# The sandwich kernel: the 1018 pieces of its first part in another order

## The chip, the cores and the metric

The kernel runs on one core of a Trainium2 chip. A core has five engines, each with its own in-order instruction queue: TensorE (PE in the profile; PEld is its weight load, which overlaps PE), VectorE (DVE), ScalarE (ACT), GpSimd (POOL) and SyncE (SP, which here only issues DMAs). Matrix products write into PSUM banks; DVE and ACT read them from there into SBUF. Engines wait for each other through semaphores. The metric is the device time of one execution in microseconds (us); times of several executions are given as a median.

## The reference, cut to what matters

Two batches of 2048 tokens with 256 channels pass through a first attention with three branches and then through two layers of local attention with a gated feed-forward network.

```python
h0 = layernorm(x, eps=1e-5)                              # (2, 2048, 256), input of the first part
gates = sigmoid(h0 @ Wg + bg); gates /= gates.sum(-1) + 1e-6
compressed = h0.reshape(2, 512, 4 * 256) @ Wc + bc        # one row for each 4 tokens
comp_out = attend(compressed)                            # 512 rows, put at the first 512 tokens
idx = sort(top_k(h0 @ Ws + bs, 128))                     # 128 tokens of each batch
sel_out = attend(h0[idx])                                # 128 rows, put at the first 128 tokens
win_out = attend(windows of 64 at stride 32)[:2048]      # first 2048 rows
out = 0.5 * (concat(comp_out*g0, sel_out*g1, win_out*g2) @ Wo + bo) + 0.5 * h0
x = x + layernorm(layernorm(out, eps=1e-6), eps=1e-5)    # end of the first part
y = layernorm(x, eps=1e-5)                               # input of the second part
for l in range(2):
    y = y + local_attention(shift(y) @ wqkv[l]) @ wo[l]  # 8 heads, blocks of 128, rotary with xpos
    a, g = split(layernorm(shift(y)) @ w1[l] + b1[l])
    y = y + (a * gelu(g)) @ w2[l] + b2[l]
result = x + layernorm(y, eps=1e-5)
```

`attend(t)` is softmax attention of t's queries against t's keys and values, with Wq, Wk, Wv.

## The kernel before, in words

The tokens lie as 8 groups g of 4 tiles of 128 rows (X[g] raw, Y[g] normed), 4 groups per batch. The kernel has two parts, with different PSUM pools: the first (lines 334 to about 905) has three banks pa, two pb, two pc and one po; the second has pa=2, pb=2, pc=4.

**How the first part is ordered.** A wrapper around the engines (class Engine, line 134, and class Notes, line 152) does not issue the operations of the first part when the code calls them; it notes them. Consecutive operations on one engine form a *piece*; `cut()` starts a new one, as does every step given to `do(f, ...)` (line 862). There are 1018 pieces. At the end

```python
with tc.manual_schedule():
    nc.give_out(int(i) for i in FIRST.split())
```

issues the pieces in the order in which their numbers stand in the string FIRST (line 41). Tiles and banks are taken when a piece is issued (class Later, line 104). No scheduler changes anything behind that, so the in-order queue of each engine is the subsequence of its own pieces in FIRST. In the profile every operation of the first part carries the line of give_out, L173, and every operation of the second part the line L147, so the tile names tell them apart.

**Steps of the first part**, with the pieces that the prediction speaks of:

- `first.turn` (53 on PE; 54, 55): turns the bias vectors, whose last row va waits for a DMA of bv; `later_on.turn` (223 on PE, 224 on DVE) does so for the second part.
- `open_moments(g)` (79 and 80 for g=1; 96/97, 114/115, 131/132, 148/149, 165/166, 183/184 for g=2 to 7): the statistics on DVE, then the reciprocal root and the shift on POOL. Group 0 has one such step for each tile (56 to 63).
- `open_norm(g)` (64 on DVE for g=0, 81, 98, 116, ... on ACT): X to Y.
- `open_turn(g)`: transposes of Y on PE in two halves (68 and 65 for g=0, 85 and 82 for g=1, ...), copies to xnT on DVE and ACT (66, 69, ...), and rearranged copies "perm" on POOL (70 and 67, 87 and 84, 104 and 101, 122 and 119).
- `open_products(g)`: gates and scores (71 and 73 for g=0, 88 and 90 for g=1, 106 and 108 for g=2) and the products of perm with Wc (75 and 77; 92 and 94; 110 and 112; 129 and 127), which give the compressed rows cT.
- `value_weights`, `value_biases` (205 to 222): products of Wv and Wo.
- the search for the 128 largest scores by counting, as rounds between DVE and PE (pieces 225 to 283 or so).
- `selected(b)` (line 686): numbers of the rows, an indirect DMA on POOL's queue that gathers them (330 for the second batch), their norm, transposes, queries, keys, values and attention (331 to 353 for the second batch).
- `compressed_open(b)` (line 665; 402 to 417 for the second batch): queries (406 on PE, 407 on DVE into qTc), keys (kTc), values (412 to 417, into cv). `compressed(b, i)` (line 674): scores (418 on PE for tile 0, 426, 434, 442 for the next), softmax and product.
- for each of 16 pairs i of windows: `win_qk`, `win_v`, `win_score`, `win_turn`, `win_out`, `win_add` and `win_close` (lines 735 to 860). `win_turn` turns the probabilities PW on PE to wpT, `win_out` multiplies them with the values VW and adds the result to Y (z) with statistics; `win_add` norms z on ACT, adds it to X on POOL and takes the statistics of X; `win_close` norms X to Y on ACT, the output of the first part. For pair 10, `win_add` is 833 to 840 (835 and 838 statistics on DVE, 839 on POOL, 840 on DVE) and `win_close` 841 and 842 on ACT; for pair 11 they are 864 to 871 (869, 871 on DVE, 870 on POOL) and 872, 873; for pair 15 `win_out` ends with 997 to 1002, `win_add` is 1003 to 1010, and `win_close` 1011 and 1012.

**The second part** has its own written-out order (a list of places with two more order strings), issued after the first. Its first operations turn tiles of Y on PE, copy them to h on ACT and multiply h with wqkv. The queues run on across the border, so ACT's first copy of h stands behind ACT's last piece of the first part.

Of the kernel before, what the change touches and what calls it, by code (L numbers as in the profile page):

```python
# [38 lines left out]


FIRST = """
2 27 6 3 23 0 1 4 5 7 8 9 10 56 205 24 11 40 25 60 12 57 13 58 14 61 62 15 16 206 59 26 63 64 68 17 28 79 65 69
70 53 66 18 80 19 54 55 71 20 21 22 72 67 81 29 73 74 30 85 96 31 75 86 87 32 77 114 97 33 82 98 78 115 83 102
34 76 148 84 116 88 35 99 92 131 149 36 89 103 37 90 94 104 150 93 91 100 38 132 105 165 120 39 117 121 41 219
101 133 42 106 43 95 122 118 44 112 45 183 46 107 119 220 47 48 110 166 49 50 113 51 52 184 108 1013 167 134 109
111 1014 123 135 1015 137 1016 136 1017 207 129 124 185 125 209 126 127 130 138 210 139 208 200 201 154 151 155
146 156 152 128 153 140 147 144 141 142 171 143 145 157 172 163 173 158 161 164 168 162 215 169 174 170 159 189
216 160 186 190 175 187 191 460 176 188 177 192 178 462 461 179 193 283 194 196 180 195 204 202 181 225 197 203
226 213 227 228 456 182 214 229 457 458 230 450 459 231 232 451 354 233 234 235 454 236 452 237 455 238 453 211
239 240 241 212 466 242 463 221 243 467 464 244 222 198 245 246 468 247 465 199 217 248 497 249 218 355 250 494  # L50
251 362 252 360 469 363 472 498 495 253 361 524 254 499 496 526 255 525 503 256 500 527 491 257 470 522 258 493
471 492 259 523 475 260 356 261 476 262 357 358 263 264 265 359 378 266 267 368 379 268 380 369 528 269 382 270
529 386 383 381 271 387 394 272 388 273 390 389 274 395 391 364 275 396 366 276 397 365 277 398 278 592 367 279
593 384 280 598 385 399 281 599 400 282 284 473 533 288 285 401 536 286 392 537 534 474 538 535 542 539 287 393
289 477 290 530 321 478 291 532 501 504 567 292 596 319 479 502 505 293 531 597 506 294 480 295 508 507 561 484
481 485 509 540 370 563 482 562 541 510 568 486 569 545 371 543 594 546 372 564 595 296 661 511 297 373 515 603
544 573 547 662 516 298 600 548 512 299 602 665 513 300 601 549 604 301 517 666 309 302 550 605 565 303 310 554
307 609 304 555 305 308 514 663 551 306 518 556 566 311 570 664 552 606 312 519 571 667 313 607 572 520 314 553
608 315 576 316 612 668 574 557 636 521 577 633 317 634 736 318 635 558 639 320 560 575 322 637 737 483 578 613
323 734 487 638 325 559 642 324 735 326 579 732 327 488 580 610 328 489 611 738 329 614 330 490 581 615 739 617  # L60
733 616 643 677 674 582 618 669 585 583 678 671 675 619 670 584 640 707 673 586 331 704 672 332 679 620 808 708
621 641 333 645 809 644 622 705 334 646 631 374 706 806 375 335 709 632 338 710 807 340 713 339 647 587 624 702
341 676 625 648 344 588 703 626 342 649 336 345 343 623 376 337 627 650 589 654 628 408 651 655 377 629 680 652
630 656 591 683 414 409 653 402 590 415 657 658 346 660 403 410 659 347 348 681 406 411 349 682 686 407 350 404
351 687 352 405 684 416 353 685 688 417 742 689 748 744 743 740 690 749 750 412 741 691 754 745 692 413 426 695
746 693 747 696 751 697 711 418 427 712 428 694 716 419 698 430 717 714 776 420 810 431 429 421 715 422 699 811
718 777 700 434 719 701 423 778 720 752 435 755 773 721 436 424 774 753 725 437 756 722 782 726 775 759 425 723
438 727 757 724 812 758 728 432 814 813 729 731 730 442 433 439 760 783 761 440 443 784 444 762 766 446 445 441
763 804 767 447 764 768 788 805 779 789 876 780 765 815 877 818 781 816 769 448 817 819 785 820 821 824 770 786
849 449 771 846 787 850 772 790 847 825 851 843 791 848 822 880 845 823 792 826 844 829 852 881 827 793 855 882  # L70
794 828 797 795 853 878 884 883 798 830 874 879 854 831 796 858 875 799 856 948 859 800 916 949 832 888 857 950
801 836 889 917 802 837 860 803 913 861 918 890 885 915 914 919 862 886 922 944 951 920 887 863 921 946 891 864
925 945 865 894 892 223 224 893 895 947 866 897 867 896 958 898 833 899 868 955 834 900 923 952 924 926 901 956
954 959 928 927 953 988 929 957 985 960 930 989 983 902 990 931 906 903 907 961 986 932 984 962 987 963 964 967
904 933 965 968 937 934 938 966 994 969 935 939 995 970 991 971 936 992 993 940 972 997 996 973 869 999 976 998
974 977 1000 870 941 978 1001 942 975 943 1002 979 871 1006 905 1003 1007 980 872 908 1004 981 1008 982 909 1005
873 838 1009 910 835 912 1010 911 839 1011 1012 840 842 841
"""


# [1374 lines left out]
```

## Time and profile before

| | us |
|---|---|
| time, median of 3 (lowest, highest) | 1560.8 (1560.66, 1562.59) |
| the profiled execution, its own time | 1561.83 |
| its span | 1560.1 |
| PE busy | 1502.4 (96%) |
| DVE busy | 1068.3 (68%) |
| ACT busy | 758.9 (49%) |
| POOL busy | 740.2 (47%) |
| granted PE clock, mean | 0.991 |
| last matmul of the first part ends | 228.12 |
| last ACT operation of the first part ends | 238.00 |
| first product with wqkv starts | 238.51 |

The profiled execution's time is 1.7 us more than its span, which runs from its first to its last instruction. How to read the profile: a line of the timeline has the start, the duration, the engine, the line, the operation, the tiles (out<-in) with their shapes, the count of operations run together, and in square brackets how long the engine had been idle and which operation released it. A line of the waits has the engine and tile that waited, the engine and tile waited for, and then the total, the number and the longest of these waits. In the page's slices each digit is the busy share of 1/40 of the span in tenths.

### The profile page before, as it was taken

How to read it: one execution, taken by the hardware profiler on the slowest of the kernel's cores; microseconds unless marked ns; L12 is line 12 of the kernel's file. 1: busy time of each engine (PE TensorE's matmuls, PEld its weight loads, DVE VectorE, ACT ScalarE, POOL GpSimd, SP SyncE). 2: the span in 40 equal slices, each digit the busy share in tenths (PEclk: the TensorE clock that was granted, in tenths of full speed). 3: DMA queues.
4: the chain of work that ended last, by engine and by line, in shares of the span. 5: the costliest groups of instructions: out<-in, count | busy, mean ns of one | idle time of the engine just before them, and what ended most of it. 6: DMA issues, size and time to landing. Idle time of an engine off the chain costs nothing.

```text
span 1560.1 us, 32507 instructions
## 1 busy us (share of the span) xinstructions
PE 1502.4 (96%) x12344; PEld 980.8 (63%) x12344; DVE 1068.3 (68%) x3139; ACT 758.9 (49%) x2213; POOL 740.2 (47%) x906
## 2 busy tenths in 40 slices
PE   7999967999999999999999999999999999999998
PEld 6877743566666666655555566666666665655554
DVE  6588784777888888844545368888888886454553
ACT  4336554677766776611111156677776765111110
POOL 7205256766666666510111166666666762232333
PEclk9999988999999999999999999999999999999999
DMA  7000001100000000101000010000000000001000
GB/s 227 1 1 8 1 18 37 33 6 8 5 9 5 8 5 8 52 8 28 14 17 0 1 41 30 9 5 9 5 9 5 6 8 8 15 31 31 21 24 31
DMA packets 32990, 30.76 MB, mean 20 GB/s; under 512 B 5634, under 2 KB 31172, under 8 KB 32836
## 3 DMA queue, kind: packets, MB, share of 16 engines
q1 hardware_dynamic: 32644, 28.17, 5.9%
q8 instruction: 98, 1.61, 0.4%
q0 software_dynamic: 192, 0.52, 0.1%
q14 instruction: 56, 0.46, 0.1%
HBM read 20.30 MB, written 4.19 MB: 16 GB/s over the span
## 4 chain that ended last, share of the span: by engine, by line
PE 76%; DVE 3%; POOL 2%; ACT 1%; issue 1%; DMA 0%; SPq 0%; POOLq 0%; ACTq 0%; DVEq 0%
PE pa L147 29%; PE pb L147 24%; PE pc L147 23%; DVE rr L147 1%; POOL rr L147 1%; DVE prob L147 1%; POOL ss L147 1%; DVE Y L147 0%; DVE hh L147 0%; ACT prob L147 0%; DVE ss L147 0%; ACT probT L147 0%; ACT sq L147 0%; DVE u L147 0%; DMA sh<-Y 0%
## 5 line engine op out<-in xcount | busy, mean ns | idle before, releaser
L147 PE MATMUL pa<-wqkv,h 128*128 128x512 f32 x768 | 370.3, 605 | 15.3 <-ACT h L147 11.3
L147 POOL TENSOR_TENSOR rr<-rr 128x256 f32<-128x256 f32 x256 | 184.4, 751 | 307.1 <-DVE rr L147 243.9
L147 ACT ACTIVATE ge<-pa,vb 128x512 f32<-128x512 f32 (+1 forms) x107 | 66.8, 626 | 363.1 <-PE pa L147 328.2
L147 ACT ACTIVATE prob<-prob,off 128x192 f32<-128x192 f32 (+2 forms) x512 | 224.8, 442 | 17.9 <-DVE off L147 17.0
L147 PEld LDWEIGHTS pa<-wqkv,h 128*128 128x128 f32 x768 | 132.1, 191 | 128.9 <-issue 104.3
L147 POOL TENSOR_TENSOR ss<-ss,mhalf 128x16 f32<-128x16 f32 x64 | 187.3, 2926 | 0.8
L147 ACT COPY probT<-pb 128x384 f32<-128x384 f32 (+1 forms) x256 | 119.2, 469 | 120.2 <-PE pb L147 117.2
L147 PE MATMUL pa<-hh,w 128*128 128x512 f32 x368 | 171.5, 593 | 0.0
L147 DVE SCALAR_TENSOR_TENSOR u<-pb,vb,ge 128x512 f32<-128x512 f32 x73 | 54.6, 751 | 165.0 <-PE pb L147 159.7
L147 DVE CUSTOM_DVE_ANT_0 prob<-pc,mask_loc 128x192 f32<-128x192 f32 (+2 forms) x512 | 148.8, 346 | 26.2 <-PE pc L147 20.4
L147 DVE TENSOR_TENSOR rr<-pa,cs 128x1024 f32<-128x1024 f32 x128 | 151.4, 1217 | 21.1 <-ACT sq L147 18.9
L147 PE MATMUL pc<-w,u 128*128 128x256 f32 (+1 forms) x896 | 164.6, 383 | 0.0
L147 PEld LDWEIGHTS pc<-w,u 128*128 128x128 f32 (+1 forms) x896 | 129.0, 173 | 47.8 <-issue 32.7
L147 PE MATMUL pb<-hh,w 128*128 128x512 f32 x292 | 137.3, 592 | 1.4 <-DVE u L147 1.4
L147 POOL TENSOR_TENSOR rr<-rr,ss 128x512 f32<-128x512 f32 x128 | 133.1, 1059 | 2.8
L147 DVE TENSOR_TENSOR prob<-prob,den 128x768 f32<-128x768 f32 x128 | 128.1, 1001 | 5.0
L147 PEld LDWEIGHTS pb<-ident,prob 128*128 128x128 f32 x752 | 87.9, 141 | 61.0 <-issue 31.2
L147 ACT ACTIVATE sq<-pa 128x512 f32<-128x512 f32 x128 | 75.6, 592 | 98.1 <-PE pa L147 93.5
L147 PE MATMUL pb<-ident,prob 128*128 128x128 f32 x752 | 118.3, 278 | 5.1 <-DVE prob L147 4.1
L147 PE MATMUL pb<-wo,oT 128*128 128x256 f32 x512 | 121.4, 380 | 0.2 <-DVE ss L147 0.2
L147 POOL TENSOR_SCALAR r<-mv 128x1 f32<-128x1 f32 (+1 forms) x48 | 9.3, 193 | 228.7 <-DVE mv L147 226.3
L147 PE MATMUL pc<-kr,qT 64*64 64x192 f32 (+2 forms) x2688 | 108.7, 287 | 2.2 <-ACT qT L147 2.2
(255 smaller groups left out, 2483.4 us busy)
## 6 DMA issues: line engine op xcount, KB each, us to landing
cs<-in_rope_dram SPq DMA_DIRECT2D x32, 128.0 KB
out_dram<-res SPq DMA_DIRECT2D x32, 128.0 KB
w<-in_L_ffn_w_dram SPq DMA_DIRECT2D x6, 640.0 KB
X<-_attn_hidden_states_dram SPq DMA_DIRECT2D x7, 512.0 KB
sh<-Y SPq DMA_DIRECT2D x16, 224.0 KB
wqkv<-in_L_ffn_wqkv_dram SPq DMA_DIRECT2D x2, 1536.0 KB
Wc<-in_L_attn_Wc_dram SPq DMA_DIRECT2D x1, 1024.0 KB
wo<-in_L_ffn_wo_dram SPq DMA_DIRECT2D x2, 512.0 KB
```

Of the source, the lines that this page charges most:

```text
L147: return f(*a, **k)
```

## The change

The string FIRST holds the same 1018 numbers in another order. Nothing else differs: the operations, their shapes, the pools and the second part's orders are the same. The order of the DMAs that SP issues is the same too. The diff, whole:

```diff
@@ -39,42 +39,42 @@
 FIRST = """
-2 27 6 3 23 0 1 4 5 7 8 9 10 56 205 24 11 40 25 60 12 57 13 58 14 61 62 15 16 206 59 26 63 64 68 17 28 79 65 69
-70 53 66 18 80 19 54 55 71 20 21 22 72 67 81 29 73 74 30 85 96 31 75 86 87 32 77 114 97 33 82 98 78 115 83 102
-34 76 148 84 116 88 35 99 92 131 149 36 89 103 37 90 94 104 150 93 91 100 38 132 105 165 120 39 117 121 41 219
-101 133 42 106 43 95 122 118 44 112 45 183 46 107 119 220 47 48 110 166 49 50 113 51 52 184 108 1013 167 134 109
-111 1014 123 135 1015 137 1016 136 1017 207 129 124 185 125 209 126 127 130 138 210 139 208 200 201 154 151 155
-146 156 152 128 153 140 147 144 141 142 171 143 145 157 172 163 173 158 161 164 168 162 215 169 174 170 159 189
-216 160 186 190 175 187 191 460 176 188 177 192 178 462 461 179 193 283 194 196 180 195 204 202 181 225 197 203
-226 213 227 228 456 182 214 229 457 458 230 450 459 231 232 451 354 233 234 235 454 236 452 237 455 238 453 211
-239 240 241 212 466 242 463 221 243 467 464 244 222 198 245 246 468 247 465 199 217 248 497 249 218 355 250 494
-251 362 252 360 469 363 472 498 495 253 361 524 254 499 496 526 255 525 503 256 500 527 491 257 470 522 258 493
-471 492 259 523 475 260 356 261 476 262 357 358 263 264 265 359 378 266 267 368 379 268 380 369 528 269 382 270
-529 386 383 381 271 387 394 272 388 273 390 389 274 395 391 364 275 396 366 276 397 365 277 398 278 592 367 279
-593 384 280 598 385 399 281 599 400 282 284 473 533 288 285 401 536 286 392 537 534 474 538 535 542 539 287 393
-289 477 290 530 321 478 291 532 501 504 567 292 596 319 479 502 505 293 531 597 506 294 480 295 508 507 561 484
-481 485 509 540 370 563 482 562 541 510 568 486 569 545 371 543 594 546 372 564 595 296 661 511 297 373 515 603
-544 573 547 662 516 298 600 548 512 299 602 665 513 300 601 549 604 301 517 666 309 302 550 605 565 303 310 554
-307 609 304 555 305 308 514 663 551 306 518 556 566 311 570 664 552 606 312 519 571 667 313 607 572 520 314 553
-608 315 576 316 612 668 574 557 636 521 577 633 317 634 736 318 635 558 639 320 560 575 322 637 737 483 578 613
-323 734 487 638 325 559 642 324 735 326 579 732 327 488 580 610 328 489 611 738 329 614 330 490 581 615 739 617
-733 616 643 677 674 582 618 669 585 583 678 671 675 619 670 584 640 707 673 586 331 704 672 332 679 620 808 708
-621 641 333 645 809 644 622 705 334 646 631 374 706 806 375 335 709 632 338 710 807 340 713 339 647 587 624 702
-341 676 625 648 344 588 703 626 342 649 336 345 343 623 376 337 627 650 589 654 628 408 651 655 377 629 680 652
-630 656 591 683 414 409 653 402 590 415 657 658 346 660 403 410 659 347 348 681 406 411 349 682 686 407 350 404
-351 687 352 405 684 416 353 685 688 417 742 689 748 744 743 740 690 749 750 412 741 691 754 745 692 413 426 695
-746 693 747 696 751 697 711 418 427 712 428 694 716 419 698 430 717 714 776 420 810 431 429 421 715 422 699 811
-718 777 700 434 719 701 423 778 720 752 435 755 773 721 436 424 774 753 725 437 756 722 782 726 775 759 425 723
-438 727 757 724 812 758 728 432 814 813 729 731 730 442 433 439 760 783 761 440 443 784 444 762 766 446 445 441
-763 804 767 447 764 768 788 805 779 789 876 780 765 815 877 818 781 816 769 448 817 819 785 820 821 824 770 786
-849 449 771 846 787 850 772 790 847 825 851 843 791 848 822 880 845 823 792 826 844 829 852 881 827 793 855 882
-794 828 797 795 853 878 884 883 798 830 874 879 854 831 796 858 875 799 856 948 859 800 916 949 832 888 857 950
-801 836 889 917 802 837 860 803 913 861 918 890 885 915 914 919 862 886 922 944 951 920 887 863 921 946 891 864
-925 945 865 894 892 223 224 893 895 947 866 897 867 896 958 898 833 899 868 955 834 900 923 952 924 926 901 956
-954 959 928 927 953 988 929 957 985 960 930 989 983 902 990 931 906 903 907 961 986 932 984 962 987 963 964 967
-904 933 965 968 937 934 938 966 994 969 935 939 995 970 991 971 936 992 993 940 972 997 996 973 869 999 976 998
-974 977 1000 870 941 978 1001 942 975 943 1002 979 871 1006 905 1003 1007 980 872 908 1004 981 1008 982 909 1005
-873 838 1009 910 835 912 1010 911 839 1011 1012 840 842 841
+2 6 0 27 3 23 40 4 5 28 24 1 7 25 8 9 10 56 11 58 12 57 60 13 14 62 61 15 16 26 59 79 63 17 205 64 80 68 206 18
+53 65 19 81 54 55 20 66 21 85 22 67 29 30 69 71 86 70 77 96 72 31 87 32 114 75 97 33 82 98 76 73 115 74 102 83
+34 78 131 84 116 88 35 99 92 100 132 36 103 165 89 37 209 90 106 104 210 133 207 38 94 93 166 91 183 39 41 107
+120 208 101 167 42 117 43 105 219 118 44 184 45 95 110 148 46 121 47 185 48 119 49 112 50 122 51 111 52 1013 220
+149 129 1014 113 1015 1016 1017 150 127 130 108 137 109 128 123 138 134 139 124 215 135 136 125 154 216 126 151
+155 146 152 200 156 201 153 144 147 163 145 140 164 161 141 142 157 162 143 171 158 168 172 159 186 169 173 189
+187 175 190 174 170 160 450 176 188 177 192 178 179 193 191 283 194 196 195 180 202 204 181 225 197 203 226 451
+458 227 460 459 228 454 461 182 462 229 456 230 455 213 231 457 232 214 354 233 234 235 211 236 237 238 212 452
+239 491 240 453 241 492 463 242 493 466 217 464 467 243 468 494 465 355 244 218 497 245 221 246 356 222 498 495
+469 472 247 496 362 499 248 357 524 249 363 503 250 500 525 470 358 251 471 252 475 359 253 360 254 476 522 361
+255 256 523 378 257 258 259 379 198 260 380 261 382 381 262 199 383 394 263 264 265 395 386 266 396 267 398 387
+268 399 368 269 388 526 369 270 390 389 527 397 271 364 272 366 273 365 274 367 384 275 276 277 385 391 598 278
+279 599 528 280 592 529 281 593 392 282 288 473 533 284 536 534 393 285 535 537 400 286 538 542 539 474 287 401
+477 290 530 478 504 289 532 291 479 321 501 596 531 480 370 292 319 484 502 481 485 505 597 482 486 293 506 371
+508 561 507 372 540 594 562 509 563 543 567 595 294 541 564 295 544 373 545 565 568 547 546 569 510 600 566 548
+665 602 570 661 549 666 601 573 571 550 606 662 296 667 572 551 297 607 511 576 608 483 603 515 552 298 663 512
+604 516 577 605 668 299 513 574 633 554 517 487 636 664 634 300 738 635 637 555 514 638 301 642 518 739 303 302
+307 612 304 309 519 308 556 520 305 310 521 736 306 488 575 311 489 609 578 312 490 553 613 732 313 737 579 557
+315 734 316 314 733 580 639 317 558 735 610 674 581 559 318 320 611 582 322 614 323 615 585 583 617 616 560 640
+586 324 631 677 632 671 641 587 584 643 669 673 644 588 325 374 672 670 618 326 645 375 647 327 589 619 702 678
+675 679 646 707 676 704 591 620 806 590 680 624 705 683 808 706 708 625 703 621 710 684 709 328 626 622 376 809
+713 329 623 807 330 648 402 627 377 649 628 681 748 629 403 404 630 682 685 749 331 750 688 754 332 405 711 650
+686 712 651 408 687 654 652 333 655 653 334 409 714 776 656 745 335 657 410 689 336 658 690 338 337 659 716 411
+339 691 340 660 746 342 341 747 344 717 343 692 346 695 345 693 810 751 347 696 777 715 778 406 694 348 782 811
+349 697 718 407 698 418 719 699 720 426 419 701 700 721 420 773 722 421 427 725 723 422 775 350 442 726 724 423
+774 428 727 351 755 728 414 429 443 430 415 444 352 729 412 431 353 445 731 740 730 413 416 741 742 417 424 743
+744 752 434 425 753 756 757 435 759 758 783 812 436 437 432 814 784 813 438 433 779 760 439 804 780 761 446 781
+440 805 785 762 447 766 786 818 763 441 767 787 815 819 448 764 820 768 765 816 824 769 817 846 449 849 821 788
+770 847 876 789 848 772 790 877 852 825 843 771 791 822 880 845 823 792 826 850 829 844 851 793 827 881 855 882
+794 828 797 795 856 878 884 830 798 853 874 879 883 831 854 796 858 875 799 950 832 800 857 836 859 888 833 916
+837 860 951 889 917 834 801 890 913 861 918 803 919 915 894 885 862 920 895 922 921 948 914 802 863 925 944 864
+886 835 867 865 946 838 887 868 949 891 866 839 892 947 223 893 945 896 897 869 899 898 870 955 958 900 923 952
+924 926 901 956 954 959 928 927 871 930 957 929 983 960 985 873 988 931 872 989 961 932 990 964 962 902 965 994
+906 984 903 963 907 986 966 967 987 953 933 904 969 991 934 995 968 937 935 970 938 992 993 971 939 997 936 972
+940 996 976 998 999 973 977 1000 974 941 1001 978 943 975 942 1002 979 840 1006 908 1003 1007 980 842 905 1004
+982 1008 981 909 1005 841 224 1009 910 911 1010 912 1012 1011
 """
```

The first 200 numbers are the same set in both orders, and so are the first 840.

## The prediction

> Pieces are called by their number in the order. All times are microseconds (us) from the start of the profiled span.
>
> **What bounds the kernel now.** First the page: the slices say where TensorE (PE) is not full. One slice is 1560.1 / 40 = 39.0 us; the first part is the first six.
>
> ```profile
> PE 1502.4 (96%) x12344; PEld 980.8 (63%) x12344; DVE 1068.3 (68%) x3139; ACT 758.9 (49%) x2213; POOL 740.2 (47%) x906
> ...
> PE   7999967999999999999999999999999999999998
> ...
> PEclk9999988999999999999999999999999999999999
> ```
>
> PE is busy 96% of the span. Of the first part, only the first slice (7) and the two at 195 to 273 us (6 and 7) leave it room, and the granted clock also sags there. Next, windows of 20 us over that part (columns: length, PE, PEld, DVE, ACT, POOL busy, granted clock, DMA share, GB/s):
>
> ```profile
> 0.00:20.00 20.00, 10.56 (x60) 7.79 (x61) 11.54 (x53) 5.36 (x10) 13.67 (x39) 1.00 0.85 269
> ...
> 160.00:180.00 20.00, 19.74 (x85) 13.26 (x84) 13.34 (x50) 9.93 (x27) 4.08 (x8) 1.00 0.00 1
> 180.00:200.00 20.00, 20.00 (x104) 16.29 (x103) 16.07 (x63) 12.79 (x35) 7.30 (x14) 1.00 0.00 0
> 200.00:220.00 20.00, 16.57 (x86) 12.34 (x85) 16.60 (x71) 12.99 (x39) 8.85 (x17) 0.99 0.07 17
> 220.00:240.00 20.00, 7.01 (x15) 3.70 (x16) 13.65 (x51) 10.04 (x20) 12.48 (x25) 0.50 0.05 18
> ```
>
> From 20 to 200 PE loses 18.96 + 19.91 + 19.74 against 60, that is 1.4 us in all. An order can hardly gain there; it can only lose. From 200 to 240 PE is idle 3.43 + 12.99 = 16.4 us. The waits of PE in the first 330 us name the releasers:
>
> ```profile
> PE pa L147 <- ACT h L147: 11.3, 4, 10.0
> PE pa L173 <- DVE Y L173: 7.6, 3, 6.5
> PE pb L173 <- DVE PW L173: 3.6, 3, 1.6
> ...
> PE pa L173 <- DMA va<-in_L_attn_bv_dram: 1.3, 1, 1.3
> ...
> PE pc L173 <- POOL perm L173: 0.9, 1, 0.9
> ```
>
> The 10.0 us wait is the seam, and the timeline shows what it is made of:
>
> ```profile
> 227.06 1.06 PE L173 MATMUL pb<-VW,wpT 98*128 98x256 f32 x2
> ...
> 234.51 2.08 ACT L173 ACTIVATE Y<-X,CLOSE 128x256 f32<-128x256 f32 x4 [0.60 <-DVE CLOSE L173]
> ...
> 236.16 0.71 DVE L173 SCALAR_TENSOR_TENSOR CLOSE<-mv,CLOSE 128x2 f32<-128x2 f32 x1 [0.89 <-POOL h L147]
> 236.91 1.09 ACT L173 ACTIVATE Y<-X,CLOSE 128x256 f32<-128x256 f32 x2 [0.33 <-DVE CLOSE L173]
> 238.02 0.43 ACT L147 COPY h<-pb 128x128 f32<-128x128 f32 x2
> 238.51 7.80 PE L147 MATMUL pa<-wqkv,h 128*128 128x512 f32 x12 [9.96 <-ACT h L147]
> ```
>
> The last matmul of the first part ends at 228.12. The second part's first product needs h, copied by ScalarE (ACT), whose queue is in order: the copy starts only when the last closing norm of the first part is done, at 238.00. So ACT's last closing norm ends the first part, not PE.
>
> **The change part by part.** No instruction is added or removed, and SP's DMA order is unchanged; only the order within the queues of PE, DVE, ACT and POOL moves. After 200 pieces (PE at about 57 us) and again after 840 pieces (about 198) both orders have issued the same set of pieces, so the change is three independent stretches, each costed against the same start.
>
> *First stretch, 0 to 57.* Moments 79 (2.0 us of DVE) move ahead of norm 64, and norm 81 ahead of copy 69 on ACT; turn 53, which waits for the DMA of va (11.51), moves ahead of the second half 65 of the first transposes. On POOL copies 70 and 67 swap. Walked with the trace's durations: va at 11.5 and 65 (1.06) bring PE to 12.7, transposes 85 to 14.4, gates 71 to 15.5; then the products wait for perm copy 70, done near 15.7 behind 67 (1.10). They start near 15.8 instead of 15.46, and piece 88 near 22.05 instead of 21.80: +0.25. Further on POOL's moments 132 (1.53) and 166 (1.60) stand ahead of perm copy 101, and 184 ahead of 119 and 122. The present wait for perm (0.88) goes; in its place piece 110 waits some 0.45 and piece 129 some 0.40. Sum 0.25 - 0.88 + 0.45 + 0.40 = +0.2. Bounds: -0.7 if both new waits are covered (0.25 - 0.88), +1.5 if POOL's 1.6 us of moments is late once more ahead of a perm copy (0.22 + 1.6, less the 0.3 of slack that copies 122 and 136 show). The value-weight transposes (207 and 209, 0.22 each) move from 35.4 and 37.5 to about 25, PE time for PE time: nothing.
>
> *Second stretch, 57 to 198.* The gather of the second batch's selected rows (piece 330, POOL's queue) moves from place 552 to 618, and its chain on PE (334 to 352) some 10 to 15 us later; window outputs of tiles 6 and 7 move as much earlier; v-products 412, 414, 416 and 740, 742 move later. What moves is PE work among PE work and costs nothing while each operand is ready. The top-k rounds keep matmuls between each count and the next; the tightest, 250 to 253 and 277 to 279, could show up to 0.3. One place has lost its cover. Piece 406 makes the queries of the compressed part, DVE piece 407 evicts them, and scores 418 need them. The present rows, in PE's timeline:
>
> ```profile
> 159.12 1.88 PE L173 MATMUL pa<-cT,Wq 128*128 128x512 f32 x4
> ...
> 170.32 1.88 PE L173 MATMUL pc<-kTc,qTc 128*128 128x512 f32 x4
> ```
>
> They are 170.32 - 161.00 = 9.3 us apart. In the new order only piece 718 (0.44) stands between. Eviction 407 takes 0.76, plus about 0.1 for each of two handovers (161.00 to 161.03 and its like), less 0.44: 0.5 if DVE is free. DVE has 694, 782, 349 and 697 (0.52 + 0.61 + 0.23 + 0.53 = 1.9) just ahead of it, over the 1.72 of piece 406 itself and what stands before it; I add 0.6 for that backlog: 1.1. Against it the 0.26 at 172.46 goes. Net +0.8; bounds 0 (DVE ahead, other rows of 418's bank later anyway) and +2.5 (all of DVE's 1.9 in the way, and 0.3 each at two top-k rounds). Behind 418 on PE stand 426 and the rest, so every us is lost to all.
>
> *Third stretch, 198 to the seam.* In the present order the closing of window pair 10 is left to the end: stats 838 and 835 (0.62 + 0.64) lie at 233.8 to 235.0, POOL 839 (0.97) at 235.16, DVE 840 at 236.16 (0.71, as a line shown has it), norms 842 and 841 at 236.91 to 238.00. Stats 869 (0.64, at 226.17) and norms 872, 873 of pair 11 are late too. The new order puts 835, 838, 839, 869, 870, 871, 872 and 873 to about 208 to 217, in DVE, POOL and ACT time beside PE work; 840, 842 and 841 go a few pieces forward. The cover: DVE is busy 16.60 of 20 from 200 to 220, so 1.9 us more there fits in 3.4 idle, not freely. Two steps follow. (a) The pure tail: ACT now ends after norms 1012 and 1011, which ended at 236.58: 238.00 - 236.58 = 1.42 gained. (b) The chain ahead of it, PE to DVE to PE over tiles 14 and 15 (962, 967, 969, 997, 999, then 1000): walked with the rows' durations, without 869 and with 961, 964 first, 928 starts near 213.9 (214.31), 962 near 218.1 (218.87), 969 at 221.0 (222.31), 997 at 224.2 (226.04), and statistics 1000 end at 227.7 instead of 229.39: 1.7. From there POOL sets the pace: 1009 ended at 235.07 and would at 233.4 to 233.6, DVE 1010 at 233.8, and four norms end at about 234.95. That is 238.00 - 234.95 = 3.05, of which 1.42 is (a) and 1.6 is (b). Bounds: 1.5 (only the tail) and 5 (all seven PE gaps between 210.95 and 226.04, which come to 6.1 us, shrink by half instead of by a quarter).
>
> The granted clock is half from 219.4 to 243.3, as trace rows show: a wqkv product takes 0.86 until 243.3 against 0.605 in the mean. If the fall and the return move with the work, nothing changes; each product more or fewer at half clock is 0.26. The return came 4.8 us after 238.51. I allow 1 either way.
>
> The Trainium skill, "TensorE: Matmul & The Clock Gate", Part 1, says that full rate comes back after about 3.4 us of activity in a free-running window and that the phase varies between runs. By that rule an estimate of this return would lie 3.4 to 6.8 us after the products start, so up to 2 us later or 1.4 earlier than here; it changes no term, and the 4.8 above agrees.
>
> Behind the seam queues and work are as before, and PE is full again from about 280 us; I carry the shift through whole.
>
> **Sum.** +0.2 + 0.8 - 3.05 = -2.05, or -2.1. The profiled execution (span 1560.1, 1561.83 in all) would come to 1559.7; it lies 1.0 above the median of 1560.8, so the median goes to 1558.7. A measurement of this kernel can tell about 0.2%, 3.1 us, from no change.
>
> **Rivals.**
> 1. *The earlier stretches cost nothing and the seam gives all.* For it: both earlier losses hang on evictions that in their present place are early by several us. Against it: the 0.44 between 406 and 418 is less than one eviction. Sum -0.7 + 0 - 3.05 = -3.8, to -5 with more closed gaps; take -4.5: 1556.3.
> 2. *Slower: the order runs DVE into the dense middle.* Between 160 and 180 DVE is busy 13.34 and between 180 and 200 it is 16.07. The new order takes work for DVE from the seam (1.9) and puts windows 6 and 7 ahead of the compressed scores. If 407, 415, 413 and 417, each now evicted long before use, all come late behind window work, each costs one eviction and handover with a window piece ahead: 0.8 + 0.9 = 1.7 each, 6.8 in all, and the seam's -3.05 and +0.4 of start leave +4.2: 1565. It decides once these waits pass 3.1 + 3.1 = 6 us. For it: those four evictions and their readers lie within 20 places. Against it: DVE has idle time of 6.7 us in the first of these windows.
> 3. *The seam gain is swallowed.* DVE 908, 905, 1008, 1005, 1010 and POOL 979 to 1009 still follow the last statistics; if PE's gaps only move, (b) is nothing, and 1.42 less 1.0 is left against 1.0 of clock: about 1561, no change.
>
> **How the numbers follow.** Forecast 0.38 (own range 1557 to 1560.5; some 0.07 of it beyond 0.2%), rival 1 0.29 (faster), rival 3 0.11 (same), rival 2 0.22 (0.02 of it within 0.2%). Faster 0.07 + 0.29 = 0.36; same 0.31 + 0.11 + 0.02 = 0.44; slower 0.20. The range goes from 1554.5 (rival 1's -5 with 1 of clock) to 1565.5 (rival 2), leaving out the ends of both, less than 0.2.
>
> **What would show it.** Right: the wait of PE for h is still about 7 to 10 us, but the first h copy starts near 235 to 236, the last norm before it being one of pair 15 (1011), and PE from 60 to 200 shows one new wait of about 1 for DVE qTc. The wait for perm near 30 is split in two smaller ones. Wrong: several waits of PE for DVE tiles qTc, kTc, cv or wpT of over 2 us together between 140 and 200; or a first h copy at 238 plus the earlier losses; or a first product later than 16.5.

## The result, and the profile after

The changed kernel takes 1559.07 us (median of 16, 1557.23 to 1559.73) against 1562.42 us for the kernel before on the same chip (median of 16, 1560.5 to 1563.5). The ratio is 0.9978, with a 95% interval of 0.9971 to 0.9986: 3.4 us faster, between 2.2 and 4.5. The forecast was 2.1 us faster.

The profiled execution of the changed kernel took 1559.31 us with a span of 1557.6; before it was 1561.83 and 1560.1. Three of the 20 us windows tell most of the story (columns as before: length, PE, PEld, DVE, ACT, POOL busy, granted clock, DMA share, GB/s):

```profile
160.00:180.00 20.00, 20.00 (x92) 14.75 (x91) 14.37 (x53) 12.67 (x34) 6.78 (x13) 1.00 0.00 1
...
200.00:220.00 20.00, 17.23 (x89) 12.59 (x87) 17.99 (x80) 14.07 (x40) 10.47 (x21) 1.00 0.12 34
220.00:240.00 20.00, 10.03 (x18) 4.52 (x17) 11.68 (x43) 9.92 (x21) 10.76 (x21) 0.51 0.00 0
```

PE did 3.7 us more from 200 to 240 than before (27.3 against 23.6), and DVE 1.4 more from 200 to 220, part of it the pieces of pairs 10 and 11 that used to lie behind 220. PE's waits in the first 330 us of the changed kernel:

```profile
PE pa L173 <- DVE Y L173: 10.1, 1, 10.1
PE pa L147 <- ACT h L147: 10.1, 4, 8.8
...
PE pb L173 <- DVE f L173: 0.9, 1, 0.9
PE pb L173 <- DVE z L173: 0.6, 1, 0.6
PE pb L173 <- DVE PW L173: 0.6, 2, 0.3
...
PE pc L173 <- POOL perm L173: 0.3, 1, 0.3
```

The transposes of PW, which waited 3.6 before, wait about 2.1 now: 0.6 under the name PW, and the 0.9 and 0.6 under f and z stand ahead of the same kind of transpose. The wait for DMA va is gone; it now lies inside the one long wait for the first Y, 10.1 instead of 6.5. The wait for h is 8.8 instead of 10.0, and it ends earlier. The seam, in the timeline of the changed kernel:

```profile
224.62 1.22 PE L173 MATMUL pb<-VW,wpT 98*128 98x256 f32 x2
...
231.83 1.09 ACT L173 ACTIVATE Y<-X,CLOSE 128x256 f32<-128x256 f32 x2 [0.33 <-DVE CLOSE L173]
...
232.66 0.73 POOL L147 TENSOR_TENSOR cs<-cs,qks 128x256 f32<-128x256 f32 x1
232.70 0.71 DVE L173 SCALAR_TENSOR_TENSOR CLOSE<-mv,CLOSE 128x2 f32<-128x2 f32 x1 [0.91 <-POOL h L147]
233.44 1.09 ACT L173 ACTIVATE Y<-X,CLOSE 128x256 f32<-128x256 f32 x2 [0.52 <-DVE CLOSE L173]
234.56 0.43 ACT L147 COPY h<-pb 128x128 f32<-128x128 f32 x2
235.04 8.23 PE L147 MATMUL pa<-wqkv,h 128*128 128x512 f32 x12 [8.78 <-ACT h L147]
```

The last norm, now one of pair 15, ends at 234.53 instead of 238.00: 3.47 earlier. The reader should keep this way of reading in mind: since the sets of pieces are the same after 200, 390 and 840 places, the start of the first PE piece behind each border divides the first part into stretches that can be compared kernel by kernel. In us, with the time from which the trace has TensorE at full clock for the first time (until then the products with perm start 0.21 apart, afterwards 0.11):

| kernel | full clock from | start to 200 | 200 to 390 | 390 to 840 | 840 to last norm |
|---|---|---|---|---|---|
| before | 18.05 | 53.47 | 57.31 | 88.40 | 38.82 |
| after | 18.88 | *53.94* | *57.84* | *87.56* | *35.19* |
| seam_only | 18.05 | 53.70 | 57.30 | 88.38 | *35.38* |
| middle_only | 17.57 | 53.36 | *57.87* | *87.58* | 38.80 |
| first_old | 20.26 | 54.55 | *57.87* | *87.58* | *35.21* |
| mixed | 17.60 | 53.05 | 57.40 | *87.59* | *35.20* |
| pair10 | 18.44 | 53.80 | 57.31 | 88.38 | 40.33 |
| rest_only | 19.25 | 54.05 | 57.32 | 88.37 | 36.93 |
| scalings | 17.98 | 53.45 | 57.32 | 88.38 | 38.39 |
| scalings10 | 18.77 | 53.81 | 57.32 | 88.39 | 39.60 |

Italics mark a stretch in the changed order; pair10 to scalings10 have orders of their own behind place 840, and mixed has the changed order from place 78 to 200. Past the first border, the same order gives the same length within 0.2 us in every execution, so differences of 0.3 can be read from single profiles there, although a time of the whole kernel can't show them.

### The profile page after: what moved, and what is told of

Read it like the earlier page. It is cut to its first block, busy times and chain, and to the rows that moved or that the text cites. A ratio compares the mean times of both kernels' runs of the same rounds, so it can differ in the third digit from the quotient of the medians.

```text
span 1557.6 us, 32502 instructions
## 1 busy us (share of the span) xinstructions
PE 1502.7 (96%) x12344; PEld 981.2 (63%) x12344; DVE 1065.8 (68%) x3139; ACT 760.2 (49%) x2213; POOL 738.7 (47%) x906
## 4 chain that ended last, share of the span: by engine, by line
PE 74%; DVE 4%; POOL 2%; ACT 1%; issue 1%; DMA 0%; SPq 0%; POOLq 0%; ACTq 0%; DVEq 0%
PE pa L147 28%; PE pb L147 24%; PE pc L147 22%; DVE prob L147 1%; DVE rr L147 1%; POOL rr L147 1%; POOL ss L147 1%; DVE Y L147 0%; ACT prob L147 0%; DVE ss L147 0%; DVE hh L147 0%; ACT probT L147 0%; ACT sq L147 0%; DVE u L147 0%; DVE off L147 0%
## 5 line engine op out<-in xcount | busy, mean ns | idle before, releaser
L147 PE MATMUL pa<-wqkv,h 128*128 128x512 f32 x768 | 370.8, 606 | 14.1 <-ACT h L147 10.1
```

The source lines that it names most:

```text
L147: return f(*a, **k)
```

## The experiments

All edits are to the order alone, unless a diff shows code. Ratios are to the kernel before, with 95% intervals.

**Stretch by stretch.**

```diff
-FIRST = before
+FIRST = before[0:840] + after[840:1018]      # seam_only
```

> Order: the first 840 pieces as before, the last 178 as in the change. Theory (the gain is made in the last stretch alone): PE starts the piece after place 840 at 199.18 as before; ScalarE's last closing norm ends 35.2 us later as in the changed kernel, at 234.4 instead of 238.0; time 3 to 3.6 us below before. Rival (the last stretch gains only because the middle has put window work earlier): last norm not before 236, time at most 2 us below before.

Measured: 1559.04 us, ratio 0.9978 (0.9969 to 0.9987), last norm 35.38 after place 840. The rival falls: the last stretch alone gives the whole gain, and doesn't need the new middle.

```diff
-FIRST = before
+FIRST = before[0:200] + after[200:840] + before[840:1018]      # middle_only
```

> Order: places 200 to 840 as in the change, the rest as before. Theory (the middle is TensorE work among TensorE work and costs nothing): piece after place 840 starts 0.2 to 0.4 us earlier than before's 199.18, last norm at 237.6 to 237.8, time 0.3 us below before, which cannot be told from no change. Rival (the forecast's term of +0.8 for the evictions that lost their cover was there and something else in the middle hid it only together with the new first stretch): piece after 840 at 199.6 or later.

Measured: ratio 0.9996 (0.9987 to 1.0005); place 840 at 198.81, 145.45 after place 200 where before has 145.71. The middle gains 0.26. It is two parts of opposite sign, 0.56 lost from 200 to 390 and 0.82 gained from 390 to 840. The rival falls: no loss of 0.8 shows at place 840.

```diff
-FIRST = after
+FIRST = before[0:200] + after[200:1018]      # first_old
```

> Order: the first 200 pieces as before, the rest as in the change. Theory (three independent stretches, the first costs 0.47): piece after place 200 starts at 53.47, after place 840 at 198.9, last norm at 234.1; time 0.5 us below the changed kernel, 3.5 to 4 below before. Rival (the stretches are not independent, the new middle needs the state of DVE and POOL that the new first stretch leaves): piece after place 840 at 199.3 or later, nothing gained on the changed kernel.

Measured: ratio 0.9978 (0.9969 to 0.9987), the same as the changed kernel's. The theory's numbers missed (place 200 at 54.55, place 840 at 200.00, last norm at 235.21), but not for the rival's reason: from 200 on every stretch is as long as in the changed kernel. It is the old first stretch that was 1.1 us longer in this execution than in the one of before. In PE's timeline of this run, the first products with perm and four products with wqkv at 253 stand out:

```profile
15.46 6.02 PE L173 MATMUL pc<-perm,Wc 128*128 128x128 f32 x32
...
253.03 3.33 PE L147 MATMUL pa<-wqkv,h 128*128 128x512 f32 x4
```

Before, the same 32 products, also from 15.46, took 4.98, and the same four wqkv products 1.98. The full clock came later here (20.26 instead of 18.05) and was lost once more from 252.37 to 255.78. So the first stretch can't be settled from one execution: over eight profiles with the old first 200 pieces, place 200 lies between 53.36 and 54.55 (mean 53.8); over three with the new ones (after, fill, fill9) between 53.94 and 54.31 (mean 54.1). Most of that spread is the clock: over the eight, place 200 starts about 0.44 later for each us that the full clock comes later (53.36 at 17.57, 54.55 at 20.26).

```diff
-FIRST = after
+FIRST = before[0:78] + after[78:200] + before[200:390] + after[390:1018]      # mixed
```

> Order: places 0 to 78 and 200 to 390 as before, 78 to 200 and 390 to 1018 as in the change; the same pieces are done at each border in both orders. Theory (independent stretches; those of the change that cost something are taken out: +0.61, +0.29, +0.24): piece after 840 starts near 198.2, last norm near 233.4, time 4.3 to 4.7 us below before and about 1 us below the changed kernel. Rival (the costs come back at the borders): last norm at 234.3 or later, time as the changed kernel.

Measured: 1558.38 us, ratio 0.9974 (0.9965 to 0.9984), place 840 at 198.04 and last norm at 233.24. The stretches add as the theory says, and the trace shows 1.3 us less than the changed kernel's 234.53. About 0.6 of that, by an estimate at 0.44 us for each us, is the full clock that came at 17.60 instead of 18.88 and not the order. The ratios differ by 0.6 us, and their intervals overlap.

**Inside the last stretch.**

```diff
-after 840: ... 888 857 ... 898 833 899 868 955 834 900 ... 1005 873 838 1009 910 835 912 1010 911 839 1011 1012 840 842 841
+after 840: ... 888 833 857 ... 917 834 802 ... 891 835 864 ... 945 838 865 ... 224 839 893 ... 1006 840 905 ... 872 842 908 ... 1005 841 873 1009 910 912 ...      # pair10
```

> Before's order with only the eight pieces of window pair 10 (833, 834, 835, 838, 839, 840, 842, 841) at their new places. Theory (this is the pure tail, 1.42 less what DVE 1010 loses when it now meets POOL's table multiply, 0.55): from the piece after place 840 to the last norm 37.7 to 38.0 instead of 38.8, so last norm 0.9 to 1.1 earlier; time about 1 us below before. Rival (the closing of pair 10 at the end is what holds the whole seam): 36 or less, time 3 us below.

Measured: ratio 1.0008 (1.0000 to 1.0017), last norm 40.33 after place 840, 1.5 later than before. Both the theory and its rival fall. Three views show the cost: DVE's timeline of this run, PE's, and PE's before.

```profile
210.02 0.42 DVE L173 BATCH_NORM_STATS2 st<-X 128x6 f32<-128x256 f32 x1
210.47 0.18 DVE L173 BATCH_NORM_AGGREGATE mv<-st 128x2 f32<-128x6 f32 x1
...
211.37 0.41 DVE L173 BATCH_NORM_STATS2 st<-X 128x6 f32<-128x256 f32 x1
211.82 0.18 DVE L173 BATCH_NORM_AGGREGATE mv<-st 128x2 f32<-128x6 f32 x1
211.92 0.13 DVE L173 RECIPROCAL f<-PW 128x1 f32<-128x1 f32 x1
212.09 0.33 DVE L173 TENSOR_SCALAR PW<-PW,f,gates 128x97 f32<-128x97 f32 x1
```

```profile
212.47 0.32 PE L173 MATMUL pb<-ident,PW 128*98 128x128 f32 x1 [1.56 <-DVE PW L173]
...
213.59 1.01 PE L173 MATMUL pc<-kW,qW 128*128 128x96 f32 x4
```

```profile
210.95 0.32 PE L173 MATMUL pb<-ident,PW 128*98 128x128 f32 x1 [0.59 <-DVE PW L173]
...
211.78 0.58 PE L173 MATMUL pc<-kW,qW 128*128 128x96 f32 x4
```

The statistics 835 and 838 of pair 10 now stand on DVE ahead of scaling 894, and PE waits 1.56 for it (0.59 before). From 213.0 to 216.4 PE then has half clock: the scores of 0.58 take 1.01. TensorE's last piece ends 2.6 later after place 840 than before (31.5 instead of 28.9). The gaps ahead of it sum to 7.7 instead of 6.5, so about half of that is waiting, and in the other half the same products took longer (23.8 of busy time instead of 22.5). Of the fourteen profiles only pair10 and scalings10, which both move pair 10 in the old order, lose the full clock before 218.9; that the waits of DVE's making cost the clock is read off the traces, not tried by itself. In this order, moving work out of the tail into a stretch in which DVE feeds PE is a loss.

```diff
-after 840: all of the new order
+after 840: the new order, pairs 10 and 11 (833 to 835, 838 to 842, 869 to 873) at their old places      # rest_only
```

> The last stretch in the new order, but with the pieces of pairs 10 and 11 (833 to 835, 838 to 842, 869 to 873) at their old places; the first 840 pieces as before. Theory (the larger part is the chain PE to DVE to PE of the last four window pairs, which the new order starts earlier): statistics 1000 end 2 to 2.5 earlier relative to place 840 than before, and the last norm 36.2 to 36.8 after it instead of 38.8. Rival (the chain is faster only because pairs 10 and 11 are out of the way): 1000 not earlier, last norm 38.4 or later.

Measured: ratio 0.9987 (0.9979 to 0.9996); statistics 1000 end 27.70 after place 840, before 30.21 and in the changed kernel 27.64; last norm at 36.93, 0.1 past the theory's window. So the chain's 2.5 us don't depend on pairs 10 and 11, and with the chain in the new order, moving the two pairs gives 1.7 more (36.93 to 35.2).

```diff
-907 961 986 932 984 962 987 963 964 967 904 933 965 968 ... 938 966 994 969 ... 970 991 971
+907 961 964 994 986 932 984 962 965 987 963 966 967 904 933 991 968 ... 969 ... 970 971      # scalings
```

> Before's order with the softmax scalings of pairs 14 and 15 brought together on DVE: 964 and 994 right after 961, 991 ahead of 968, and with them 965 right after 962 and 966 right after 963. Nothing of pairs 10 and 11 moves. Theory (PE's gaps of 1.56, 1.16 and 1.49 in the tail come from scalings that stand behind result additions on DVE): statistics 1000 end 1.5 to 2.2 earlier after place 840 than before's 30.2, last norm 37.0 to 37.4 after it instead of 38.8, time 1.4 to 2 us below before. Rival (the gain of the chain comes from the earlier pieces 853 to 930 of the stretch): 1000 at 29.7 or later, no change in time.

Measured: ratio 0.9998 (0.9989 to 1.0007); 1000 ends at 29.41, 0.80 earlier, last norm 0.43 earlier. The mechanism is there, at half the size or less that was expected; 29.41 lies between what the theory and what the rival asked for. So it isn't the whole chain. Where the rest, 1.7 of 2.5, comes from is only read off the traces: in the changed kernel 928 starts 0.61 earlier after place 840, and 930, which stands ahead of scores 988 and 985 there, 1.46 earlier. PE's gaps up to its last piece go from 6.5 to 4.0 with the new order, at the same busy time of 22.5, so the chain's gain is waiting that is gone. No run took the parts of the rest apart.

```diff
+as scalings, pair 10 at its new places, 894 behind 915 and 895 behind 862      # scalings10
```

> As scalings, and the pieces of pair 10 at their new places as in pair10, and scaling 894 with its transpose 895 moved ahead of them (894 behind 915, 895 behind 862). Theory (pair 10's statistics cost in pair10 because they stood ahead of scaling 894 on DVE; with the scalings ahead of them the move gains its tail): last norm 35.4 to 36.2 after place 840, time 2.5 to 3.3 us below before. Rival (DVE has no room for pair 10 between 205 and 217 in this order at all): 37.5 or later, not below scalings.

Measured: ratio 1.0001 (0.9992 to 1.0010), last norm 39.60 after place 840. The rival holds: even with the scalings ahead, the old order has no room on DVE for pair 10 there. The wait of 0.59 at 895 is 0.23, and 897 waits 1.42 in its place; PE is again at half clock from 213.3 to 216.8.

**The clock at the seam.** The first wqkv products run at half clock after the idle stretch. These kernels fill it (the diff is shortened: the filling piece has the number -1 in FIRST, and its bank is taken at the first product):

```diff
+        def fill():                      # one PSUM bank, never read
+            nc.tensor.matmul(warm[0], lhsT=ident, rhs=attn_w[0][:, 0, 0 : 2 * H], start=True, stop=True)
-FIRST: ... 998 999 973 ...      ... 841 224 1009 ...
+FIRST: ... 998 999 (fill x6) 973 ...      ... 223 893 224 ...      # fill
```

> The changed kernel, with six products of the identity with a slice of wqkv (128 x 512) into an unused PSUM bank after TensorE's last piece of the first part, and copy 224 right after 223 so that the bank is free. They fill the idle time and nothing reads them. Theory (the granted clock follows recent activity, and the first twelve wqkv records run at half rate because PE idles 9 us ahead): the filling takes 7 to 8.5 us, half of it at half clock; the first products start near 235.0 as before but take 5.2 to 5.6 instead of 8.2; time 2.5 to 3 us below the changed kernel. Rival (the clock returns by a window of its own, whatever the filling does, or the 1 to 2 us left idle lower it again): first products still 7.5 to 8.5, time as the changed kernel or up to 1 above where the filling runs over.

Measured: 1557.34 us, ratio 0.9964 (0.9951 to 0.9977). The profiled execution was the slowest of five, 1560.05, and shows why; PE's timeline:

```profile
226.26 6.14 PE L147 MATMUL pa<-wqkv,ident 128*128 128x512 f32 x12
...
235.68 8.33 PE L147 MATMUL pa<-wqkv,h 128*128 128x512 f32 x12 [3.06 <-ACT h L147]
```

Twelve filling records at full clock would be 5.2 (0.43 each), so the clock had risen: the trace has it full from 227.93 to 234.75. In the 3.06 us of idleness it fell, and the products were at half clock again until 241.58. The other four executions took 1556.47 to 1557.57. That the clock had stayed high in them is not shown: their granted clock over the whole span, 0.994 to 0.996, is no higher than the 0.995 of the slow one.

```diff
-FIRST = mixed
+FIRST = mixed, with (fill x6) behind 999 and 224 behind 893      # fill_mixed
```

> The same filling in the order that was tried as mixed (places 0 to 78 and 200 to 390 as before). Theory (the gains add): last norm near 233.3, first products 5.2 to 5.6 long, time about 7 us below before, the fastest of all. Rival (filling takes activity from elsewhere or meets the earlier seam): not below mixed, about 4.5 under before.

Measured: ratio 0.9970 (0.9958 to 0.9981), with two groups of times, 1555.2 to 1555.4 (two of seven) and 1558.6 to 1560.3. The theory's 7 us are not there; the median, 4.7 below before by the ratio, is not told from mixed, as the rival has it. Profiled was one of the slower group; eight of its first products took 5.20 where full clock would take 3.4 (0.43 each).

```diff
-FIRST: ... 999 (fill x6) 973 ...
+FIRST: ... 999 (fill x9) 973 ...      # fill9
```

> As fill, with nine filling products instead of six, so that PE is busy until the first h is there. Theory (in fill the 3.06 us of idleness behind the filling lowered the clock again: first products 8.33 long): filling 8.7 to 9.6 long, gap ahead of the first product under 0.6, first products 5.2 to 5.6 long, time 2.5 to 3 us below the changed kernel in every run and with less spread than fill. Rival (the clock is lowered whatever PE does there): first products 7.5 or longer; time as fill or later by what the filling runs over, up to 1.5.

Measured: 1557.66 us, ratio 0.9970 (0.9959 to 0.9982), spread 1.6 instead of 3.6. PE's timeline:

```profile
226.02 10.20 PE L147 MATMUL pa<-wqkv,ident 128*128 128x512 f32 x18
...
236.97 3.70 PE L147 MATMUL pa<-wqkv,h 128*128 128x512 f32 x8 [0.52 <-ACT h L147]
```

Eight records in 3.70 are full clock: the theory on the clock holds. But 18 records took 10.20, 2.5 more than at full clock, so the filling ran over, as the rival's second half had it: the first product began 2.03 after the last norm, where it was 0.51 in the changed kernel. That is 1.5 lost. The twelve records, with a wait of 0.30 for DVE among them, ended 5.98 after their start instead of 8.23. In this execution that leaves 0.7; by the ratios (0.9970 and 0.9978) the filling gains about 1.2, with intervals that overlap.

```diff
-FIRST = mixed
+FIRST = mixed, with (fill x9) behind 999 and 224 behind 893      # fill9_mixed
```

> The nine filling products in the order of mixed. Theory: first products 5.2 to 5.6 long, time near 1555.5, about 7 us below before. Rival: first products 7.5 or longer, time near 1558.4 as mixed.

Measured: 1556.32 us, ratio 0.9961 (0.9947 to 0.9975), the lowest of all and below both kernels of the case; last norm at 233.51, first products from 235.53, eight records in 3.70. The ratio is 0.0017 or 2.7 us under the changed kernel's; mixed (0.6) and fill9 (1.2) add up to 1.8, and the intervals don't tell these apart.

## Why the prediction was right, and where it was not

*The sum.* Forecast -2.05 to the last norm, measured -3.47. Sign and place were right: the seam carries it. The absolute forecast, 1558.7, lies within 0.4 of the measured 1559.07, and that is luck: the kernel before took 1562.42 on this chip and not 1560.8, and the change was 3.4 and not 2.1. The measured change of 0.22% lies at the border of what was counted as no change. Of the signs that it named, the wait for h of 8.8 and the last norm of pair 15 came, and the first h copy at 234.56 is a little earlier than 235; the new wait for qTc and the second wait for perm did not come. Rivals 2 and 3 did not come; rival 1's picture (no loss in the middle, the seam whole) is the nearest to what the trace shows, at a smaller size. The terms:

*First stretch, +0.2.* In the two profiles +0.47, but most of that is not the order. The full clock came at 18.88 instead of 18.05, and the 32 perm products took 5.47 instead of 4.98. The new order's three starts of place 200 (53.94 with the full clock from 18.88, 54.07 from 19.05, 54.31 from 19.71) lie 0.03 to 0.12 above what the old order has at the same clock, read between its rows of 18.77, 19.25 and 20.26. So the order costs about 0.1 by this estimate, and no run held the clock fixed. The forecast's start of the perm products (15.8) was 15.44, since the va wait costs nothing any more. Piece 88 came at 22.41, not 22.05: the products were longer, and it waits 0.52 for its operand xnT (83), which stands behind 76 and 74 on DVE. In the old order this wait is 0.35 where the products are as long (5.55 in rest_only, 6.02 in first_old). The perm waits near 30 shrank to 0.27 in all, where 0.85 was foreseen. What the term lacked is the spread: transpose 53, which waits for DMA va in the old order, started there between 11.3 and 12.0, and the perm products took 4.67 to 6.02 in runs of one order. Its lower bound is 0.25 - 0.88 = -0.63, not -0.7.

*Second stretch, +0.8.* This step failed: it measured -0.31, and -0.26 in middle_only. The named stall at 418 did not come. From the timeline of the changed kernel:

```profile
164.93 1.88 PE L173 MATMUL pa<-cT,Wq 128*128 128x512 f32 x4
...
166.86 0.74 DVE L173 TENSOR_SCALAR qTc<-pa,va 128x512 f32<-128x512 f32 x1
...
167.09 2.31 PE L173 MATMUL pc<-kTc,qTc 128*128 128x512 f32 x5
```

Product 418 starts at 167.09, with eviction 407 still running until 167.60. Scores are summed over two halves of qTc, and 407 writes only the second, which is read 0.86 later, at 167.95. DVE had no backlog either: 407 starts 0.05 after 406 ends, so the 0.6 for backlog was nothing too. The forecast counted a dependency on a whole tile where it is one on half a tile. It also took 0.1 for a handover where the row that it names, 161.00 to 161.03, has 0.03. The rest of the -0.82 from 390 on, and the +0.54 ahead, are many intervals of 0.1 to 0.4 between matmuls that have other neighbours. The largest is the old wait of 0.26 at 172.46 and what goes with it, 0.43; a new wait of 0.21 for sx at 158.29, with what goes with it, takes 0.37 of that back. No run took these apart. Rival 2's four late evictions did not happen.

*Third stretch, -3.05.* It measured -3.63, and -3.4 to -3.6 in three more kernels. The split was off. At the end of 1000 the chain (b), taken as 1.7 there, is 2.5 (rest_only). With pairs 10 and 11 still at the end, the last norm gains only 1.9 of that; moving them gives 1.7 more. Behind 1000 the changed kernel needs 7.55 to the last norm instead of 8.61, so the tail (a), taken as 1.42, is 1.1. It is there only behind the chain's new order: by itself the move of pair 10 costs 1.5 (pair10). The prediction said that DVE's room from 200 to 220 is there "not freely" and priced that at nothing; in the old order pair10 shows a price of more than the tail gives, and in the new order that price does not show. PE's gaps behind place 840 were 6.5 us and are 4.0. The seven gaps of 6.1 of its upper bound begin at 201.95; from 210.95 to 226.04 there are six, of 5.75. On the tail, DVE 1010 takes 0.71 where before it took 0.16, because now it is the last small operation that runs beside POOL's table multiply (0.73); before, 840 was. Small as it is, this takes 0.55 from the tail as it was forecast.

*The shift carried through whole.* Not in the profiled execution: the shift of -3.47 is -3.03 after the first products, -2.08 at 316 us and -2.5 at the end of the span. The first 0.43 is the granted clock: it returned 5.7 us after the first product instead of 4.8, and the 12 records took 8.23 instead of 7.80. The Trainium skill, "TensorE: Matmul & The Clock Gate", Part 1, says that the window runs free and the phase changes from run to run; the times of return in the ten kernels without filling, 3.0 to 5.7 after the first product, vary as it says. The 3.0 of first_old lies below the 3.4 that the prediction's estimate had as the least. The next 1.0 is a single DVE operation, in the changed kernel

```profile
308.32 1.03 POOL L147 TENSOR_TENSOR rr<-rr,ss 128x512 f32<-128x512 f32 x1
308.32 2.06 DVE L147 TENSOR_SCALAR off<-top 128x4 f32<-128x4 f32 x1
```

and before

```profile
311.33 1.03 POOL L147 TENSOR_TENSOR rr<-rr,ss 128x512 f32<-128x512 f32 x1
311.35 1.05 DVE L147 TENSOR_SCALAR off<-top 128x4 f32<-128x4 f32 x1
```

An operation that takes 0.17 in other places of the same program takes 1.05 beside one POOL operation and 2.06 beside two. In 13 of the 14 profiles it took 1.02 to 1.05, those of the other kernels with the new last stretch among them, so 2.06 belongs to this execution and not to the change. The medians differ by 3.35, between 2.2 and 4.5 by the interval, which is compatible with the seam's -3.47 whole; the times can't say it closer. The Trainium skill, "SBUF — State Buffer", section "SBUF: two separate sides", says that VectorE and GpSimd share a port pair; for VectorE operations of certain kinds, the engine that starts first holds it for its whole instruction and the other waits. The lengths of 1.05 and 2.06, against 1.03 for one POOL operation, agree; that this operation is of such a kind no row shows.

## What to carry to other kernels

Where two orders have issued the same set of work at some places, cut them there: the stretches add, each can be tried alone, and the profile resolves 0.1 to 0.3 us where a time can't. Moving closing work forward out of a tail pays only where the engine that does it has room at that place beside feeding the bound engine: the same eight pieces cost 1.5 us in one order, and with their like of pair 11 gave 1.7 in another. When a wait is forecast from an eviction, look which half of the tile is read first. And before a few tenths at the start are put down to an order, look when the clock rose in each execution.

## What the runs showed of the hardware that was not expected

In all fourteen profiles every stretch of full or half clock that the trace has, the last one aside, is a multiple of 3.41 us long: the first full one 201.39 (59 times) or 194.56 (57 times), the half one at the seam 23.89 before and 20.48 after (7 and 6 times). Where this grid lies against the kernel changes with the execution: the first rise came between 17.57 and 20.26, and the first stretch moved by 1.2 us with it.

The clock fell with gaps far below 3 us: in pair10 at 213.0, after waits of 0.20, 0.16 and 1.56 between 210 and 212.5, and in first_old at 252.37, after several waits of 0.3 to 1.1. An idle time of 3.06 at the seam was enough in fill to lose a clock that six filling products had just won. And the cost of one 0.17 us DVE operation beside POOL was 0.9 or 1.9 us: in the 13 profiles POOL's operation started 0.015 to 0.04 us ahead of it, in the one with 2.06 both started within 0.001.
